# Bias and router loads moved to turn 7, the second half's entry and the router stretched, the experts moved by four slots

## The chip, the cores and the metric

The kernel runs on one core of one Trainium2 chip. A core has engines that run beside each other, each taking its own queue of instructions in order: TensorE (PE: matmuls and transposes; its weight loads are listed apart as PEld), VectorE (DVE), ScalarE (ACT) and GpSimd (POOL). SyncE (SP) does no arithmetic here; it issues every DMA of the kernel, also in order. An instruction that has to wait for a semaphore holds up everything behind it in its own queue. The metric is the time of one execution on the device in microseconds (us); lower is better.

## What is computed

Four sequences of 256 tokens with 256 features go through two residual layers. The first is a gated delta net, a linear attention computed in chunks; the second is a mixture of experts. Cut to what matters:

```
x = x + layernorm(attn(layernorm(x)))      # four sequences of 256 tokens, 256 features
x = x + layernorm(moe(layernorm(x)))

attn: q, k, v, z  = x @ W_qkvz             # 16 query/key heads, 32 value heads, 128 wide
      b, a        = x @ W_ba
      q, k, v     = silu(causal_conv4(...))
      beta, g     = sigmoid(b), -exp(A_log) * softplus(a + dt_bias)
      for each chunk of a head:
          T      = inverse(I + stril(k_beta @ k.T * decay))
          v_new  = T @ v_beta - (T @ (k_beta * exp(g))) @ state
          out    = (q * exp(g)) @ state + (q @ k.T * decay) @ v_new
          state  = state * exp(g_last) + (k * exp(g_last - g)).T @ v_new
      out = (norm_w * rmsnorm(out) * silu(z)) @ W_out

moe:  p     = softmax(x @ router_w + router_b)
      gates = top 6 of 32, scaled to sum 1
      out   = mean of 2 shared experts + sum over gates of gate * expert(x)
      expert(x) = relu(x @ w1 + b1) @ w2 + b2       # 256 -> 176 -> 256
```

## The kernel before, in words

All arithmetic is in 32-bit floats. The attention is cut into 32 **units**: unit u is one query/key head with its two value heads, over two of the four sequences. Units 0 to 15 cover the first half of the tokens, 16 to 31 the second half. A unit goes through stages written as Python generators:

- `weights` issues the loads of the projection weights `w`, of `wz` (gate) and of `wo` (output projection).
- `decays` loads the unit's cumulated gates, tile `gw`, from the DRAM tensor `g_rows` (L301), one copy to all partitions. POOL adds a mask (L307) and ACT takes exponentials (L317).
- `prepare` does the projection (`pj`, L357), the convolution on DVE (L367), transposes for the norms, and the products `pk` (L409, L433), which DVE combines with `gw` into the tile `am` (L413, L436). It then writes the diagonal 16 x 16 blocks of `am` to DRAM as `mb`, eight DMAs (L453).
- `blocks`, once for two units (u odd), reads these back as `wm` (L474), inverts them on DVE, writes the result to DRAM as `db` (L522), and loads it into the tiles `diag[0]` and `diag[1]`, one for each unit, eight DMAs each (L528). In the profile the two tiles have one name, `diag`.
- `solve` builds the inverse of the unit's matrices from these blocks on PE (`py`, `pd`, `pdT`, L545). Its first matmul, `py<-diag,e`, waits for the unit's `diag`.
- `gate` and `finish` compute `pz`, the solution `pu` and `pm`, the output `po`, its norm, the transposes `pth`, and the projection `pp` (L690), which DVE adds to `acc`.

Beside the units run five other stages. `entry(h)` normalises half h of the tokens, transposes it into `xT` (`pt_a`), computes the gates from `pba`, and writes them to `g_rows` (L260). `small` loads the router's weights `rw` and `rb`, the expert biases `b2s`, and the biases `b1`. The last come in as `b_raw`, go out to a DRAM tensor `b1f` in another order, one element of 4 bytes at a time (128 x 34 in one DMA and 48 x 34 in another: 5,984 elements), and come back as `b1s` in two more DMAs. The read of `b1s` has to wait until both writes of `b1f` have landed. `post(h)` forms the residual, normalises it, transposes it into `xT` again and computes the router's gates, mostly on DVE. `experts(h)` runs over 47 groups of hidden features: matmul `ph` (L849), ACT's relu (L852), DVE's product with the gates (L858), matmul `py` (L869), and at its end the last norm and the store.

**The order of the work** is written out by hand. A turn is nine slots, `at(turn, slot) = turn * 9 + slot`, and unit u starts at `at(u, 0)`. Each `yield` in a stage names the place at which the instructions behind it are to stand, and a heap takes the stages' pieces in the order of their places. This fixes the queues of PE, ACT, DVE and POOL instruction by instruction. It says nothing of times: a piece with a later place stands further back in its engine's queue. SP's queue is ordered by the framework's own scheduler, from these places and its estimate of when a DMA can go; `tc.issue_after(x)` makes the DMAs of its block stand behind x in SP's queue. `places(start, step)` gives a stage with many pieces a place every `step` slots.

Tiles come from pools with few buffers, so a DMA into a tile may have to wait until the earlier content has been read. The expert weights `we` use the buffers of `am` (four), the products of gates and hidden features those of `gw`, and so on.

Of the kernel before, what the change touches and what calls it, by code (L numbers as in the profile page):

```python
# [17 lines left out]
HQK, HV, HD = 16, 32, 128  # L18
# [13 lines left out]
def at(turn, slot):  # L32
    return turn * SLOTS + slot
# [30 lines left out]
def gated_delta_net_moe(  # L64
# [26 lines left out]
    def bank(tag, shape, name):  # L91
        return psum.tile(shape, F32, tag=tag, name=name)
# [13 lines left out]
    def load_x(name, h):  # L106
        xns[h] = u1.tile([P, NL, D], F32, tag="xn", name=f"xn_{name}_{h}")
        nc.sync.dma_start(xns[h], tokens(x_in, h))
# [45 lines left out]
    def places(place, step):  # L154

        while True:
            yield place
            place += step

    def layernorm(at_, src, dst, eps, name, tiles=range(NL)):  # L160

        n = len(tiles)
        st = ln.tile([P, NL, 6], F32, tag="st", name=f"st_{name}")
        mv = ln.tile([P, NL, 2], F32, tag="mv", name=f"mv_{name}")
        rs = ln.tile([P, NL], F32, tag="rs", name=f"rs_{name}")
        for i, t in enumerate(tiles):
            yield next(at_)
            nc.vector.bn_stats(st[:, i, :], src[:, t, :])
            nc.vector.bn_aggr(mv[:, i, :], st[:, i, :])
        nc.vector.tensor_scalar(rs[:, :n], mv[:, :n, 1], eps, None, ALU.add)  # L170
        nc.gpsimd.tensor_tensor(rs[:, :n], rs[:, :n], nhalf[:, :n], ALU.pow)
        for i, t in enumerate(tiles):
            yield next(at_)
            nc.vector.tensor_scalar(
                dst[:, t, :], src[:, t, :], mv[:, i, 0:1], rs[:, i : i + 1], ALU.subtract, ALU.mult
            )

    def transposed(at_, src, h, name):

        for k in range(2):  # L180
            yield next(at_)
            pt = bank("ms", [P, NL, P], f"pt_{name}_{k}")
            for i in range(NL):
                nc.tensor.transpose(pt[:, i, :], src[:, i, k * P : (k + 1) * P], ident)
            nc.scalar.copy(xT[:, k, h * T : (h + 1) * T], pt.rearrange("p a b -> p (a b)"))
# [82 lines left out]
    state = [{} for _ in units]  # L268
# [436 lines left out]
    groups = [(i, min(P, nh - i)) for i in range(0, nh, P)]  # L705
# [13 lines left out]

    def small():  # L720

        yield at(3, 0)
        nc.sync.dma_start(rw, router_w.rearrange("(k p) e -> p k e", p=P))
        nc.sync.dma_start(rb, router_b.partition_broadcast(P))
        nc.sync.dma_start(b2s, b2)
        raw = u1.tile([P, 13, NL * HV // 2], F32, tag="temp", name="b1_raw")
        b1f = dram.tile([nh], F32, name="b1f")
        for i, rows in enumerate((slice(0, P), slice(P, DH))):
            n = rows.stop - rows.start
            nc.sync.dma_start(raw[:n, i, :NE], b1[rows, :])  # L730
            nc.sync.dma_start(b1f.rearrange("(e h) -> h e", h=DH)[rows, :], raw[:n, i, :NE])
        yield at(5, 0)
        full = nh // P
        nc.sync.dma_start(b1s[:, :full], b1f[: full * P].rearrange("(i p) -> p i", p=P))
        nc.sync.dma_start(b1s[: nh - full * P, full:], b1f[full * P :].rearrange("(i p) -> p i", i=1))

    def post(h, at_):

        tl = slice(h * NL, (h + 1) * NL)
        a = acc[:, tl, :]  # L740
        yield next(at_)
        load_x("b", h)
        xn = xns[h]
        yield from layernorm(at_, a, a, 1e-5, f"b_{h}")
        for i in range(2):
            yield next(at_)
            c = slice(2 * i, 2 * i + 2)
            nc.vector.tensor_tensor(a[:, c], xn[:, c], a[:, c], ALU.add)
        yield from layernorm(at_, a, xn, 1e-5, f"c_{h}")
        yield from transposed(at_, xn, h, f"c_{h}")  # L750
        yield next(at_)
        plg = bank("ms", [P, NL, NR], f"plg_{h}")
        for t in range(NL):
            for k in range(2):
                nc.tensor.matmul(
                    plg[:, t, :],
                    xT[:, k, h * T + t * P : h * T + (t + 1) * P],
                    rw[:, k, :],
                    start=(k == 0),
                    stop=(k == 1),  # L760
                )
        temp = u1.tile([P, 13, NL * HV // 2], F32, tag="temp", name=f"route_{h}").rearrange("p a b -> p (a b)")
        used = [0]

        def part(*shape):
            n = shape[0] * (shape[1] if len(shape) > 1 else 1)
            got = temp[:, used[0] : used[0] + n]
            used[0] += n
            return got.rearrange("p (a b) -> p a b", a=shape[0]) if len(shape) > 1 else got

        lg, pr, rest, gates, top = (part(NL, n) for n in (NR, NR + 2, NR + 2, NE, 8))
        mx, sm = part(NL), part(NL)
        nc.vector.tensor_tensor(lg, plg, rb.unsqueeze(1).to_broadcast([P, NL, NR]), ALU.add)
        yield next(at_)
        nc.vector.tensor_reduce(mx, lg, AX.X, ALU.max)
        nc.vector.tensor_tensor(lg, lg, mx.unsqueeze(2).to_broadcast([P, NL, NR]), ALU.subtract)
        yield next(at_)
        nc.scalar.activation(lg, lg, AF.Exp)
        yield next(at_)
        nc.vector.tensor_reduce(sm, lg, AX.X, ALU.add)  # L780
        nc.vector.reciprocal(sm, sm)

        nc.vector.memset(pr, -1.0)
        nc.vector.tensor_tensor(
            pr[:, :, :NR], lg, sm.unsqueeze(2).to_broadcast([P, NL, NR]), ALU.mult
        )
        yield next(at_)
        for t in range(NL):
            nc.vector.max(top[:, t, :], pr[:, t, :NR])
        nc.vector.memset(top[:, :, TOPK:], -1.0)  # L790
        yield next(at_)
        for t in range(NL):
            nc.vector.match_replace(rest[:, t, :], top[:, t, :], pr[:, t, :], 0.0)
        yield next(at_)
        nc.vector.tensor_tensor(gates[:, :, :NR], pr[:, :, :NR], rest[:, :, :NR], ALU.subtract)
        nc.vector.tensor_reduce(sm, gates[:, :, :NR], AX.X, ALU.add)
        nc.vector.reciprocal(sm, sm)
        nc.vector.tensor_tensor(
            gates[:, :, :NR], gates[:, :, :NR], sm.unsqueeze(2).to_broadcast([P, NL, NR]), ALU.mult
        )  # L800

        nc.vector.memset(gates[:, :, NR:], 1.0 / NS)
        yield next(at_)
        gTs[h] = u1.tile([NE, 2 * 3 * P], F32, tag="gr", name=f"gT_{h}")[:, :T]
        pgt = bank("ms", [NE, NL, P], f"pgt_{h}")
        for t in range(NL):
            nc.tensor.transpose(pgt[:, t, :], gates[:, t, :], ident)
        nc.scalar.copy(gTs[h], pgt.rearrange("p a b -> p (a b)"))
        nc.sync.dma_start(gate_rows[h], gTs[h])
# [7 lines left out]
    def experts(h, start):  # L817
# [56 lines left out]
                    stop=(i + 1 == n),  # L874
                )

        LAG, EARLY = 2, 12
        for i in range(-EARLY, n + LAG):
            yield start + i
            if 0 <= i + EARLY < n:  # L880
# [40 lines left out]
    def begin(place, stage):  # L921
        heapq.heappush(parts, (place + next(stage), len(begun), place, stage))
        begun.append(stage)

    stages = [
        entry(0, places(-9, 0.3), places(6.8, 0.1)),
        entry(1, places(at(6, 0), 0.7), places(at(10, 0), 0.7)),
        small(),
        post(0, places(at(HQK + 4, 6), 0.7)),
        experts(0, at(2 * HQK + 2, 0)),  # L930
        post(1, places(at(2 * HQK + 4, 5), 0.5)),
        experts(1, at(2 * HQK + 2, 0) + len(groups)),
    ]
    for stage in stages:
        begin(0, stage)
    for u in range(len(units)):
        for stage in [weights, decays, prepare, gate, finish, solve] + [blocks] * (u % 2):
            begin(at(u, 0), stage(u))

    E = mybir.EngineType  # L940
    with tc.manual_schedule(engines={E.PE, E.Activation, E.DVE, E.Pool}):
        while parts:
            _, number, place, stage = heapq.heappop(parts)
# [52 lines left out]
```

## Time and profile before

| | |
|---|---|
| median of 3 runs | 1556.27 us (1556.08 to 1556.82) |
| the profiled execution's own time | 1556.75 us |
| its span in the profile | 1554.9 us |
| PE busy | 1454.9 us, 94% of the span |
| DVE, ACT, POOL busy | 839.8, 867.0, 464.8 us |
| moved by DMA | 126.51 MB, 81 GB/s over the span |
| packets | 232329, of which 159190 under 512 B |

The page of the profile cuts the span into 40 slices of some 39 us. Units fill the first 28 of them or so; from there the experts join, and the last ten are theirs almost alone. The trace can be asked for a timeline of each engine, for windows (busy time of each engine in a stretch), for waits (who waited for whom, put down to the releaser that came last) and for the chain of waits that ended last.

### The profile page before, as it was taken

What the parts mean: (1) busy time and instruction counts of PE and PEld (TensorE: products, weight loads), DVE (VectorE), ACT (ScalarE), POOL (GpSimd) and SP (SyncE); (2) the same over time, 40 slices, a digit from 0 to 9 for tenths busy, and PEclk for the clock granted to TensorE, in tenths of its full rate; (3) what the DMA queues carried; (4) which work ended last, traced back from release to release, by engine and by line L of the source; (5) the groups of instructions that cost most, each with busy time, mean ns of one, the idle gap of its engine ahead of it and who ended that gap; (6) DMA issues with size and microseconds to landing.
All of it is one profiled execution on the core that took longest, in us unless ns stands there. A gap on an engine that the chain in (4) does not pass through costs nothing.

```text
span 1554.9 us, 30006 instructions
## 1 busy us (share of the span) xinstructions
PE 1454.9 (94%) x11652; PEld 1009.9 (65%) x11652; DVE 839.8 (54%) x1693; ACT 867.0 (56%) x2206; POOL 464.8 (30%) x306
## 2 busy tenths in 40 slices
PE   5459998999999999999999999999979999999997
PEld 3226766777777777777777777777866654444443
DVE  4375666566575756668775765767431224231212
ACT  4456667777677777766677777677523321222111
POOL 1132333343354334345424334345331110000000
PEclk8679999999999999999999999999989999999999
DMA  3521312232222323223222323223133455555521
GB/s 114 68 60 50 93 41 66 71 81 62 61 67 57 85 71 71 62 56 67 64 69 58 93 62 71 64 54 75 35 68 89 123 146 144 151 149 161 155 75 44
DMA packets 232329, 126.51 MB, mean 81 GB/s; under 512 B 159190, under 2 KB 201528, under 8 KB 232188
## 3 DMA queue, kind: packets, MB, share of 16 engines
q1 hardware_dynamic: 232188, 124.59, 31.2%
q8 instruction: 93, 1.52, 0.4%
q14 instruction: 48, 0.39, 0.1%
HBM read 116.82 MB, written 7.70 MB: 80 GB/s over the span
## 4 chain that ended last, share of the span: by engine, by line
PE 72%; DVE 11%; ACT 7%; DMA 4%; issue 3%; SPq 2%; POOL 0%; POOLq 0%; DVEq 0%; ACTq 0%
PE ph L849 10%; PE py L869 10%; PE pj L357 10%; PE pp L690 6%; PE pz L331 4%; PE pd L545 4%; PE pdT L545 4%; DVE c L367 3%; PE po L634 3%; PE py L545 3%; PE pk L409 3%; PE pu L621 3%; ACT junko L643 2%; PE po L638 2%; PE pk L433 2%
## 5 line engine op out<-in xcount | busy, mean ns | idle before, releaser
L367 DVE SCALAR_TENSOR_TENSOR c<-pj,cw,c 128x510 f32<-128x510 f32 (+2 forms) x384 | 286.1, 745 | 168.9 <-ACT c L365 159.8
L654 POOL TENSOR_TENSOR rs<-rs,nhalf 128x4 f32<-128x4 f32 x64 | 78.0, 1220 | 678.6 <-DVE rs L650 473.3
L357 PE MATMUL pj<-xT,w 128*128 128x512 f32 x512 | 250.3, 613 | 5.1 <-DVE c L367 5.0
L852 ACT ACTIVATE h<-ph,b1s 128x512 f32<-128x512 f32 (+1 forms) x94 | 64.6, 687 | 241.5 <-PE ph L849 241.3
L849 PE MATMUL ph<-xT,we 128*128 128x512 f32 (+1 forms) x376 | 177.6, 595 | 0.7 <-ACT d L586 0.7
L365 ACT ACTIVATE c<-pj,cw 128x512 f32<-128x512 f32 x128 | 87.5, 685 | 161.6 <-PE pj L357 161.6
L869 PE MATMUL py<-hg,we 128*128 128x512 f32 (+1 forms) x376 | 176.4, 593 | 0.0
L858 DVE TENSOR_TENSOR hg<-h,gb 128x512 f32<-128x512 f32 (+1 forms) x94 | 65.7, 700 | 175.5 <-ACT h L852 168.3
L553 POOL TENSOR_TENSOR e<-am,cst 64x1024 f32<-64x1024 f32 x64 | 151.0, 2359 | 2.4
L357 PEld LDWEIGHTS pj<-xT,w 128*128 128x128 f32 x512 | 96.1, 198 | 79.3 <-issue 75.5
L646 DVE TENSOR_TENSOR hm<-po,sz 128x512 f32<-128x512 f32 x64 | 43.9, 686 | 179.1 <-ACT junko L643 177.2
L869 PEld LDWEIGHTS py<-hg,we 128*128 128x128 f32 (+1 forms) x376 | 71.3, 190 | 90.5 <-issue 88.6
L690 PE MATMUL pp<-wo,hT 128*128 128x256 f32 x512 | 123.2, 384 | 3.6 <-ACT hT L685 3.6
L331 PE MATMUL pz<-wz,xT 128*128 128x256 f32 x512 | 122.1, 382 | 0.0
L849 PEld LDWEIGHTS ph<-xT,we 128*128 128x128 f32 (+1 forms) x376 | 69.4, 189 | 77.8 <-issue 76.2
L690 PEld LDWEIGHTS pp<-wo,hT 128*128 128x128 f32 x512 | 98.0, 192 | 32.8 <-ACT hT L685 17.0
L331 PEld LDWEIGHTS pz<-wz,xT 128*128 128x128 f32 x512 | 93.3, 192 | 10.7 <-issue 0.5
L409 PE MATMUL pk<-c 128*128 128x512 f32 x128 | 73.0, 653 | 29.0 <-DVE am L413 22.0
L413 DVE SCALAR_TENSOR_TENSOR am<-pk,br,gw 128x512 f32<-128x512 f32 x128 | 89.9, 743 | 18.7 <-ACT gw L317 17.7
L317 ACT ACTIVATE gw<-gw,ng 128x256 f32<-128x256 f32 (+1 forms) x256 | 98.7, 447 | 1.5 <-POOL gw L307 1.1
L643 ACT ACTIVATE junko<-po 128x128 f32<-128x128 f32 x256 | 70.9, 277 | 48.8 <-PE po L638 34.1
L307 POOL TENSOR_TENSOR gw<-gw,cst 128x1024 f32<-128x1024 f32 x32 | 75.5, 2358 | 49.3 <-DMA gw<-g_rows 49.3
(170 smaller groups left out, 2734.5 us busy)
## 6 DMA issues: line engine op xcount, KB each, us to landing
gw<-g_rows SPq DMA_DIRECT2D x32, 768.0 KB, 5.6
w<-in_w_qkvz SPq DMA_DIRECT2D x32, 512.0 KB, 4.9
we<-in_w SPq DMA_DIRECT2D x126, 128.0 KB, 2.6
gb<-gate_rows SPq DMA_DIRECT2D x34, 256.0 KB, 3.5
wz<-in_w_qkvz SPq DMA_DIRECT2D x32, 256.0 KB, 2.7
wo<-in_w_out SPq DMA_DIRECT2D x32, 256.0 KB, 2.7
mb<-am SPq DMA_DIRECT2D x256, 8.0 KB, 1.6
db<-dd SPq DMA_DIRECT2D x16, 256.0 KB, 2.0
```

The source lines that it names most:

```text
L317: nc.scalar.activation(y, y, AF.Exp, bias=ng[:, t, h : h + 1])
L331: nc.tensor.matmul(pz[:, j].rearrange("p r e -> p (r e)"), xT[:, k, t * P : (t + 1) * P], state[u]["wz"][:, k, :], start=(k == 0), stop=(k ...
L357: nc.tensor.matmul(pj.rearrange("p b s -> p (b s)"), state[u]["w"][:, k, col * P : (col + 1) * P], xT[:, k, bp * T : (bp + 1) * T], start= ...
L367: nc.vector.scalar_tensor_tensor(y[:, :, back:], pj[:, :, : S - back], cw[:, row, 3 - back : 4 - back], y[:, :, back:], ALU.mult, ALU.add,)
L409: nc.tensor.matmul(pk, s[:, 1, b * S : b * S + P], s[:, 0:2, b * S : (b + 1) * S], start=True, stop=True)
L413: nc.vector.scalar_tensor_tensor(am[:, r, b, 0:4, :].rearrange("p (i x) c -> p i (x c)", i=2), pk, br[:, 2 * b, r : r + 1], gw[:, r, b, 0: ...
L545: nc.tensor.matmul(po[g, h, :], lhsT[g, h, :], rhs[g, h, :], start=True, stop=True)
L553: nc.gpsimd.tensor_tensor(e[g], mt[g, :, g].unsqueeze(1).to_broadcast(full), lev[g].unsqueeze(2).to_broadcast(full), ALU.mult,)
L643: nc.scalar.activation(junk, po[:, b, r, :], AF.Square, accum_out=os_[:, x, b, r : r + 1])
L690: nc.tensor.matmul(pp[:, b, :], hT[:, b, r, :], state[u]["wo"][:, r, :], start=(r == 0), stop=(r == R - 1))
L849: nc.tensor.matmul(ph[:rows], w[:, k * P : k * P + rows], xT[:, k, c], start=(k == 0), stop=(k == 1))
L869: nc.tensor.matmul(py[m], w[:rows, 2 * P + m * P : 2 * P + (m + 1) * P], hgs[i // 3][:rows, i % 3 * T : (i % 3 + 1) * T], start=False, sto ...
```

## The change

Five things change. Places first: the loads of `small`, which stood at turn 3 (and the two reads of `b1s` at turn 5), now all stand at turn 7, and in SP's queue behind the read `wm` of unit 5's blocks. `entry(1)` keeps its start at turn 6 but takes 1.4 slots from piece to piece instead of 0.7, and its second part starts at turn 12 instead of turn 10. `post(0)` too takes 1.4 slots from piece to piece. Both halves of the experts start four slots later. The expert weights are issued ten slots ahead of their group instead of twelve. (`base` is a new name for an old value.)

```
     def small():
-        yield at(3, 0)
+        yield at(7, 0)
+        with tc.issue_after(state[5]["wm"].ins):
+            small_loads()
+
+    def small_loads():
         nc.sync.dma_start(rw, router_w.rearrange("(k p) e -> p k e", p=P))
         nc.sync.dma_start(rb, router_b.partition_broadcast(P))
         nc.sync.dma_start(b2s, b2)
...
             nc.sync.dma_start(raw[:n, i, :NE], b1[rows, :])
             nc.sync.dma_start(b1f.rearrange("(e h) -> h e", h=DH)[rows, :], raw[:n, i, :NE])
-        yield at(5, 0)
         full = nh // P
         nc.sync.dma_start(b1s[:, :full], b1f[: full * P].rearrange("(i p) -> p i", p=P))
         nc.sync.dma_start(b1s[: nh - full * P, full:], b1f[full * P :].rearrange("(i p) -> p i", i=1))
...
-        LAG, EARLY = 2, 12
+        LAG, EARLY = 2, 10
...
         entry(0, places(-9, 0.3), places(6.8, 0.1)),
-        entry(1, places(at(6, 0), 0.7), places(at(10, 0), 0.7)),
+        entry(1, places(at(6, 0), 1.4), places(at(12, 0), 1.4)),
         small(),
-        post(0, places(at(HQK + 4, 6), 0.7)),
-        experts(0, at(2 * HQK + 2, 0)),
+        post(0, places(at(HQK + 4, 6), 1.4)),
+        experts(0, at(2 * HQK + 2, 4)),
         post(1, places(at(2 * HQK + 4, 5), 0.5)),
-        experts(1, at(2 * HQK + 2, 0) + len(groups)),
+        experts(1, at(2 * HQK + 2, 4) + len(groups)),
     ]
...
     for u in range(len(units)):
+        base = at(u, 0)
         for stage in [weights, decays, prepare, gate, finish, solve] + [blocks] * (u % 2):
-            begin(at(u, 0), stage(u))
+            begin(base, stage(u))
```

## The prediction

> **What bounds the kernel now.** I read the page first, then the waits of TensorE (PE), then SyncE's (SP's) queue and the windows wherever PE is idle.
>
> The page's busy times and slices:
>
> ```profile
> PE 1454.9 (94%) x11652; PEld 1009.9 (65%) x11652; DVE 839.8 (54%) x1693; ACT 867.0 (56%) x2206; POOL 464.8 (30%) x306
> ...
> PE   5459998999999999999999999999979999999997
> ...
> PEclk8679999999999999999999999999989999999999
> ```
>
> PE is the bound, idle for 100 of 1554.9 us: in slices 1 to 3, slightly in 5 to 7 and 19 to 20, in slice 30, and at the tail. The change adds and removes no arithmetic, so it can only move these gaps, or open a new one.
>
> SP's queue at the start (start, us, line, operation):
>
> ```profile
> 35.59 0.37 SPq L260 DMA_DIRECT2D g_rows<-gr  x1
> ...
> 36.81 0.38 SPq L731 DMA_DIRECT2D b1f<-b_raw  x1
> 37.43 2.81 SPq L301 DMA_DIRECT2D gw<-g_rows  x2
> 40.34 7.42 SPq L731 DMA_DIRECT2D b1f<-b_raw  x1
> 63.94 0.36 SPq L734 DMA_DIRECT2D b1s<-b1f  x1
> 64.35 4.29 SPq L735 DMA_DIRECT2D b1s<-b1f  x1
> 68.69 3.98 SPq L453 DMA_DIRECT2D mb<-am  x8
> ```
>
> The bias scatter b1f (5,984 elements of 4 bytes in two DMAs) goes out 0.6 us ahead of unit 0's and 1's gates gw; b1s then waits for it until 63.94. Who waits for gw, from POOL's and PE's timelines:
>
> ```profile
> 57.52 2.34 POOL L307 TENSOR_TENSOR gw<-gw,cst 128x1024 f32<-128x1024 f32 x1 [49.27 <-DMA gw<-g_rows]
> ```
>
> ```profile
> 61.93 2.07 PE L409 MATMUL pk<-c 128*128 128x512 f32 x2 [19.75 <-DVE am L413]
> ```
>
> The chain of waits confirms it: gw holds the path from 37.43 for 19.95 us, against a median landing of 5.6 us.
>
> SP's queue around turn 7:
>
> ```profile
> 228.82 0.34 SPq L474 DMA_DIRECT2D wm<-mb  x1
> ...
> 241.82 0.37 SPq L283 DMA_DIRECT2D wz<-in_w_qkvz  x1
> 243.15 0.34 SPq L522 DMA_DIRECT2D db<-dd  x1
> 246.50 7.69 SPq L528 DMA_DIRECT2D diag<-db  x16
> ```
>
> Windows around entry(1), in a quiet stretch, and during post(0):
>
> ```profile
> 200.00:240.00 40.00, 35.23 (x313) 27.38 (x311) 29.42 (x62) 24.30 (x67) 12.62 (x8) 0.96 0.21 63
> 240.00:280.00 40.00, 36.47 (x341) 27.60 (x341) 25.49 (x48) 30.31 (x73) 15.51 (x10) 0.96 0.28 62
> 400.00:440.00 40.00, 40.00 (x415) 31.15 (x415) 24.13 (x45) 29.46 (x77) 18.89 (x12) 1.00 0.23 57
> 720.00:760.00 40.00, 38.40 (x405) 30.23 (x400) 33.80 (x65) 25.92 (x70) 19.18 (x13) 1.00 0.28 68
> 760.00:800.00 40.00, 36.37 (x347) 28.22 (x346) 31.58 (x79) 27.08 (x68) 14.15 (x9) 0.96 0.25 67
> ```
>
> After the length come the busy times of PE, PEld, DVE, ACT and POOL, the granted clock, DMA share and GB/s. A quiet turn has no idle PE, so whatever delays PE there is paid in full.
>
> **The change part by part.** The profiled execution took 1556.75 us (span 1554.9, 1.85 around it), 0.5 above the median of the runs; the sum is made against it.
>
> *The scatter leaves the start.* Nothing then stands ahead of gw. At the median landing of 5.6 us it arrives at 43.0 instead of 57.43: 14.4 us less. If it lands only with the second gw behind it (11.2), 8.8 less. Windows of 54 to 58 us show 170 and 378 GB/s while these two loads run freely, so I take 14. Everything up to 115 us follows from gw through POOL, ACT and DVE, so the gain passes on. rw, rb, b2s and b_raw held nothing there: g_rows went out as its copy ended. b1s's 4.3 us on SP ended at 68.64, when am was ready too, so their removal is worth nothing; the cover is DVE's am.
>
> *The scatter in turn 7.* In the built program SP's order there is: wm of blocks(5), gw, rw, rb, b2s, b_raw twice, w, b1f twice, wz, b1s twice, then db and the 16 diag. So db, on which the next solve hangs, is queued behind b1s, which waits for the whole scatter. Counted from wm's issue (t0): the small issues take 3.4 us; b_raw lands behind gw's 5.6, so b1f's elements start at about t0+8. Its length: at the start the first DMA's 4,352 elements held gw for 14.4 us, 3.3 ns each, so 19.8 us for all; both DMAs with the two gw between took 36.81 to 63.94, 27.1 us. I take 23.5, as gw ran freely for part of the 27. So b1s goes out at t0+31.5; from its issue to the queue's next one took 4.75 us (63.94 to 68.69), so db at t0+36.3. From db to PE's first complete py took 7.3 us at the start (107.72 to 114.98): py at t0+43.6. In undisturbed turns py starts 23.5 us (305.87 to 329.35) or 22.7 us (442.52 to 465.22) after wm; with a pt_a transpose placed ahead of it, 24. PE, which takes its queue in order, stalls 19.5 us (16 to 23 with the ends), and ACT, DVE and the later mb all wait for PE. After its long idle at the start the granted clock was 0.50 up to the window of 66 to 68 and 1.00 in that of 70 to 72, with PE restarted at 61.93; about 6 us at half speed cost 3 more. Together +22.5 (18 to 26.5). Nothing hides it: PE has no idle time to give.
>
> A rule speaks against this step. The Trainium skill (DMA: Bandwidth & Descriptors, Rules for kernel authors) says to issue a DMA early and wait on its semaphore late. The trace's 19.95 us of gw show what early cost here, but the wait right behind b1f in turn 7 is what the rule warns of; by the rule alone, early would be free, and the move would be worth +22.5 with no gain.
>
> The same skill (TensorE: Matmul & The Clock Gate, Why this matters for your kernels) has the clock fall after some 3 us of idle, and (Part 1: The HAM clock gate) come back after about 3.4 us of work. That would make the clock's term 1.7 instead of 3, an estimate from that page; the rows above decide.
>
> *entry(1) at half the pace.* The two windows from 200 to 280 lose 4.77 + 3.53 us idle and 2 x 40 x 0.04 = 3.2 us of clock: 11.5. TensorE's waits from 195 to 265 us name its operations: pt_a on xn_a 2.3, pba on xT 1.4, and pp on ACT's hT 2.2, while ACT loads entry(1)'s tables. With 1.4 slots between steps instead of 0.7, DVE and ACT meet half the extra work per turn, and what follows the stall finds them drained. Ends: 0 (the delays stay) and 11.5; near the second, I take 10, one such wait staying. Its second half moves two turns; PE, ACT and DVE then do the same work there, and g_rows is read only from unit 16 on (turn 15): nothing.
>
> *post(0) at half the pace.* The windows from 720 to 800 lose 1.6 + 3.63 idle and 1.6 of clock, 6.8 us. DVE is busy 65 us there, 20.6 in the quiet 800 to 840. Ends 0 and 6.8; I take 4.5, since its single DVE groups stay as long as they were.
>
> *Experts four slots later, their weights two slots later still.* SP's queue at the transition:
>
> ```profile
> 1136.04 0.33 SPq L522 DMA_DIRECT2D db<-dd  x1
> 1138.54 0.38 SPq L831 DMA_DIRECT2D we<-in_w  x1
> ...
> 1145.41 3.87 SPq L528 DMA_DIRECT2D diag<-db  x8
> ```
>
> Thirteen expert loads stand between db and diag, and py waits for diag until 1150.76 though its predecessor on PE ended at 1144.95. In the new order four stand there: 1.9 us, so diag at 1140.5, landed about 1.8 after its 3.87 us of issue, at 1146.1: 4.6 us less, and some 2 of the clock (it was 0.51 from 1150 to 1155). Against it, four slots of solve and finish lose the first expert matmuls as filler; the same steps of the unit before, unfilled, show waits of 0.69 and 0.53 us (pp on hT, pth on hm), so 1.2 to 3. Net -4 (-6.5 to +5). DVE and POOL keep their work, post(1) its places, the tail its order: nothing.
>
> Sum: -14 + 22.5 - 10 - 4.5 - 4 = -10, so 1546.7 against the profiled execution and 1546.2 against the median.
>
> **The rivals.** (1) *The turn 7 wait is hidden.* If the scatter, with less beside it on the DMA engines, takes 4 us or less, py comes at t0+24 (8 + 4 + 4.75 + 7.3) and the 22.5 falls away: 1524. For it: after the gw, the second DMA's 1,632 elements had landed within some 7 us. Against: that is about 4 ns each, and 5,984 of them 24 us.
>
> (2) *Slower.* The scatter drains more slowly among turn 7's traffic than at the start, and PE stands at the same py for longer. Its price: the second DMA's 1,632 elements landed 23.6 us after their issue, two gw ahead of them included, so 14 ns each is an upper bound; at 7 ns the scatter takes 41.9 us and PE's loss grows by 18.4: 1564.6. It decides from where the stall and the clock cost 36 us (the gains of 32.5 and 3.1 more), which is a scatter of 37 us, 6.2 ns an element. For it: while the first one drained, gw's loads crawled at 14 to 38 GB/s, so each slows the other. Against: the 27.1 us at the start held two loads of 768 KB already, and turn 7 has one such ahead of it and a w of 512 KB.
>
> (3) *No change.* Should the 14 and the stall stand, but the spread steps give only half (7) and the transition nothing, the sum is +1.5: 1557.8, which cannot be told from the median; 0.2% is 3.1 us, about what a measurement can tell from no change.
>
> **How the numbers follow.** The forecast has 0.60 (own range 1538 to 1552), rival 1 0.12, rival 2 0.18, rival 3 0.10. Faster: 0.60 + 0.12 = 0.72; within 0.2%: 0.10; slower: 0.18. The range reaches from 1533 (rival 1's upper part: a stall of 9 to 10) to 1561 (rival 3, and rival 2 up to 6.5 ns an element).
>
> **What would show it.** gw landing 5 to 7 us after its issue, with the wait of pk on am near 6 instead of 19.75; in turn 7 b1s issued some 31 us after wm and one PE wait of py on diag near 20 us, clock 0.50 behind it; windows at entry(1) and post(0) nearly full; py's last long wait on diag at the transition about 1 us. The prediction is wrong if SP passes b1s without a wait of over 10 us, if PE's startup gap shrinks less than the gw wait, or if the four slots ahead of the experts show more than 5 us of idle PE.

## The result, and the profile after

The changed kernel takes 1556.2 us (median of 12 runs, 1551.84 to 1560.57), the kernel before 1555.15 in the runs beside it (median of 12). The ratio is 1.0007, with a 95% interval of 0.9994 to 1.0019: no difference. The forecast was 1546.2. The profiled execution took 1558.12 us with a span of 1556.3, 1.4 more than the span before.

The page of the changed kernel, TensorE's (PE's) busy time and its slices and clock:

```profile
PE 1459.9 (94%) x11652; PEld 1015.6 (65%) x11652; DVE 845.7 (54%) x1693; ACT 866.3 (56%) x2206; POOL 463.0 (30%) x306
...
PE   5668996999999999999999999999989999999997
...
PEclk9779998999999999999999999999989999999998
```

Slices 2 and 3 are fuller than before (6 and 6 in place of 4 and 5), slice 7 has become a hole (6, with the clock at 8, in place of 8 and 9), and the last slices look alike. So something was gained early and given back at about 250 us. To put numbers on it, both traces can be read at one landmark, the start of each unit's second key product on PE (pk_2, line 433). An undisturbed turn takes 33.6 us:

| stretch, by pk_2 of units | before, us | after, us | difference |
|---|---|---|---|
| start to unit 4 | 180.7 | 166.7 | -14.0 |
| unit 4 to 9 (scatter, entry(1)) | 184.6 | 199.3 | +14.7 |
| unit 9 to 12 (entry(1)'s second part) | 101.0 | 105.0 | +4.0 |
| unit 12 to 19 | 235.2 | 235.2 | 0 |
| unit 19 to 24 (post(0)) | 179.2 | 179.8 | +0.6 |
| unit 24 to 31 | 233.4 | 233.2 | -0.2 |
| unit 31 to the end (transition, experts) | 440.8 | 437.1 | -3.7 |

The differences add up to the 1.4 us of the spans. The start and the transition went as forecast; the stretch from unit 4 to 12 cost 18.7 more than before where the forecast had +12.5 (22.5 for the scatter less 10 for entry(1)'s pace), and post(0) gave nothing.

**The start.** SyncE's (SP's) queue, then POOL's and PE's rows that wait for gw (start, us, engine, line, operation; in brackets the idle time before it and what ended it):

```profile
35.17 0.35 SPq L260 DMA_DIRECT2D g_rows<-gr  x1
37.01 0.89 SPq L301 DMA_DIRECT2D gw<-g_rows  x2
53.67 3.65 SPq L453 DMA_DIRECT2D mb<-am  x8
```

```profile
42.52 2.34 POOL L307 TENSOR_TENSOR gw<-gw,cst 128x1024 f32<-128x1024 f32 x1 [34.21 <-DMA gw<-g_rows]
```

```profile
46.93 2.08 PE L409 MATMUL pk<-c 128*128 128x512 f32 x2 [5.03 <-DVE am L413]
```

Nothing stands between g_rows and gw any more; gw lands within 5.5 us of its issue instead of 19.95, and PE waits 5.03 us instead of 19.75.

**Turn 7.** SP's queue from wm, on the path of the next solve, to diag, which that solve needs:

```profile
213.41 0.34 SPq L474 DMA_DIRECT2D wm<-mb  x1
...
219.97 3.05 SPq L735 DMA_DIRECT2D b1f<-b_raw  x2
223.11 6.53 SPq L283 DMA_DIRECT2D wz<-in_w_qkvz  x1
241.20 0.36 SPq L737 DMA_DIRECT2D b1s<-b1f  x1
241.61 3.48 SPq L738 DMA_DIRECT2D b1s<-b1f  x1
245.19 0.38 SPq L522 DMA_DIRECT2D db<-dd  x1
```

and PE's rows at the end of it, with windows behind them (length, busy us of PE, PEld, DVE, ACT, POOL, granted clock, DMA share, GB/s):

```profile
238.65 1.14 PE L599 MATMUL pdl<-phi,y_l 64*64 64x64 f32 x16
250.78 0.44 PE L545 MATMUL py<-diag,e 64*64 64x64 f32 x2 [10.98 <-DMA diag<-db]
252.67 1.93 PE L545 MATMUL py<-diag,e 64*64 64x64 f32 x30 [1.45 <-DMA diag<-db]
```

```profile
245.00:250.00 5.00, 0.00 (x0) 0.00 (x0) 0.00 (x0) 0.00 (x0) 0.26 (x1) 0.50 0.44 66
250.00:255.00 5.00, 2.77 (x33) 2.53 (x34) 0.36 (x1) 0.00 (x0) 0.00 (x0) 0.50 0.36 34
255.00:260.00 5.00, 5.00 (x16) 3.42 (x16) 2.68 (x6) 0.00 (x0) 0.00 (x0) 0.82 0.13 19
```

b1s goes out 27.8 us after wm, db 31.8 after, and PE stands for 12.4 us at py, all other engines with it. The clock is at 0.50 until well after PE has restarted.

**Around entry(1) and post(0)** the windows should have been nearly full. They are not:

```profile
280.00:320.00 40.00, 36.32 (x334) 27.87 (x333) 31.09 (x60) 27.14 (x70) 14.49 (x9) 0.94 0.20 59
...
400.00:440.00 40.00, 37.48 (x359) 29.05 (x358) 24.46 (x44) 28.27 (x73) 19.50 (x12) 1.00 0.19 52
...
760.00:800.00 40.00, 36.82 (x352) 28.92 (x351) 30.55 (x64) 25.53 (x68) 15.22 (x10) 0.95 0.20 58
```

The first two are new losses, at places that were full before; the third is as it was.

**The transition.** SP's queue and PE's longest wait there:

```profile
1140.70 0.33 SPq L522 DMA_DIRECT2D db<-dd  x1
1142.78 0.38 SPq L834 DMA_DIRECT2D we<-in_w  x1
...
1144.70 8.80 SPq L528 DMA_DIRECT2D diag<-db  x16
```

```profile
1151.09 1.92 PE L545 MATMUL py<-diag,e 64*64 64x64 f32 x30 [1.69 <-DMA diag<-db]
```

Four expert loads instead of thirteen stand between db and diag, and py's wait is 1.69 us.

### The profile page after: what moved, and what is told of

Read it like the earlier page. It is cut to its first block, busy times and chain, and to the rows that moved or that the text cites. A ratio compares the mean times of both kernels' runs of the same rounds, so it can differ in the third digit from the quotient of the medians.

```text
span 1556.3 us, 30025 instructions
## 1 busy us (share of the span) xinstructions
PE 1459.9 (94%) x11652; PEld 1015.6 (65%) x11652; DVE 845.7 (54%) x1693; ACT 866.3 (56%) x2206; POOL 463.0 (30%) x306
## 3 DMA queue, kind: packets, MB, share of 16 engines
q1 hardware_dynamic: 232188, 124.59, 31.3%
## 4 chain that ended last, share of the span: by engine, by line
PE 69%; DVE 12%; ACT 6%; DMA 6%; SPq 3%; issue 3%; POOL 1%; POOLq 0%; DVEq 0%; ACTq 0%
PE ph L852 10%; PE py L872 10%; PE pj L357 9%; PE pp L690 5%; PE pd L545 4%; PE pdT L545 4%; PE pz L331 4%; DVE c L367 3%; PE po L634 3%; PE py L545 3%; PE pk L409 2%; PE pu L621 2%; ACT junko L643 2%; PE pk L433 2%; PE po L638 2%
## 5 line engine op out<-in xcount | busy, mean ns | idle before, releaser
L634 PE MATMUL po<-ut,am 128*128 128x128 f32 x512 | 91.1, 292 | 0.0
L634 PEld LDWEIGHTS po<-ut,am 128*128 128x128 f32 x512 | 76.8, 201 | 17.5 <-issue 15.3
```

The lines of the kernel that those rows point to most:

```text
L634: nc.tensor.matmul(po[:, b, r, :], am[:, r, b, x, :], ut[:, 0, b, r, :], start=True, stop=(x == 0))
```

## The experiments

The forecast's terms are A, the scatter leaving the start; B, the scatter in turn 7; C, entry(1) at half the pace; D, post(0) at half the pace; E, the experts four slots later. The ratios are to the kernel before, with 95% intervals. "Excess" is what a stretch takes beyond 33.6 us a turn in the profiled execution.

**One part at a time.** First the changed kernel with the small loads back where they were, and the kernel before with one of the other edits alone:

```
 # small loads back:       small() as before (turn 3 and turn 5), the rest as changed
 # entry alone:
-        entry(1, places(at(6, 0), 0.7), places(at(10, 0), 0.7)),
+        entry(1, places(at(6, 0), 1.4), places(at(12, 0), 1.4)),
 # post alone:
-        post(0, places(at(HQK + 4, 6), 0.7)),
+        post(0, places(at(HQK + 4, 6), 1.4)),
 # experts alone:           at(2 * HQK + 2, 4) for both halves, EARLY = 10
```

> The changed kernel with the small loads put back where they stood before (the scatter at the start, no wait in turn 7); the two slower paces and the later experts stay. The forecast's terms C, D and E (-10, -4.5, -4) make 18.5 us less than before: ratio 0.988. Rival theory, from the trace of the changed kernel: the slower paces only spread the same delays over more turns (entry(1) +3, post(0) +0.6) and only the transition gains (-3.7): no difference from before, ratio 1.000. In the trace the forecast wants turns of about 34 us from unit 5 to 9; the rival wants excesses of 1 to 6 us in four or five turns there.

> The kernel before with entry(1) alone at 1.4 slots a step and its second half at turn 12. Forecast: 10 us less, ratio 0.9936. Rival (spread, not saved): between 0 and 3 us more, ratio 1.000 to 1.002. A third theory, that the pace does help but the stall in turn 7 takes the gain back, wants about -10 here too and wants it lost only beside the stall.

> The kernel before with post(0) alone at 1.4 slots a step. Forecast: 4.5 us less, ratio 0.997. Rival (spread, not saved): +0.6, ratio 1.0004, with the same 11 us of excess spread over four turns in place of three.

> The kernel before with the experts four slots later and their loads ten groups ahead in place of twelve, nothing else. Forecast's term E: 4 us less, ratio 0.9974, with py's wait on diag at the transition falling from 4.0 us to about 1. Rival: the four slots without filler cost what the wait gives back: ratio 1.000, with waits of pp and pth of 3 us or more in the last attention turns.

| kernel | ratio | excess, unit 4 to 9 | unit 9 to 12 | unit 19 to 24 | unit 31 to end, us |
|---|---|---|---|---|---|
| before | 1 | 16.6 | 0.2 | 11.2 | 440.8 |
| changed | 1.0007 | 31.3 | 4.2 | 11.8 | 437.1 |
| small loads back | 0.9989 (0.9980 to 0.9997) | 11.0 | 4.3 | 11.8 | 436.9 |
| entry alone | 1.0013 (1.0003 to 1.0023) | 11.3 | 4.2 | 11.2 | 439.3 |
| post alone | 0.9985 (0.9974 to 0.9997) | 15.4 | 0.4 | 8.5 | 439.4 |
| experts alone | 0.9984 (0.9975 to 0.9993) | 16.4 | 0.3 | 9.6 | 436.9 |

C, D and E together gave 1.7 us (0.0011 of 1556), where the forecast had 18.5. Entry alone is 2 us slower, not 10 faster. Its trace shows the two halves of this: the first part saves 5 us between units 4 and 9, the second part costs 4 more between 9 and 12. (1.3 of the 5 are the second part's, which in the kernel before had begun in the turn of unit 9. The 2 us themselves are partly the start: its unit 4 begins at 182.9 us, that of before at 180.7, and the edit touches nothing there.) Post alone saves 2.3 of 4.5. The experts alone save 2.5 by the times and 3.9 by the trace: the 4 of the forecast lie at the upper end of the interval (1.1 to 3.9).

Where the first part's gain went is seen in PE's waits between units 5 and 7. In the kernel before:

```profile
227.03 0.65 PE L184 MATMUL pt_a<-cst,xn_a 128*128 128x128 f32 x2 [2.26 <-DVE xn_a L174]
234.33 2.00 PE L200 MATMUL pba<-wba,xT 128*128 128x64 f32 x16 [1.43 <-ACT xT L185]
252.66 2.75 PE L690 MATMUL pp<-wo,hT 128*128 128x256 f32 x8 [2.16 <-ACT hT L685]
260.30 1.12 PE L409 MATMUL pk<-c 128*128 128x512 f32 x2 [1.36 <-ACT junk L388]
```

With entry(1) alone at 1.4 slots:

```profile
237.11 0.27 PE L545 MATMUL pd<-y,dT 64*64 64x64 f32 x1 [2.47 <-DVE y L568]
250.00 0.66 PE L684 MATMUL pth<-cst,hm 128*128 128x128 f32 x4 [0.23 <-POOL hm L656]
251.57 1.12 PE L409 MATMUL pk<-c 128*128 128x512 f32 x2 [0.92 <-DVE am L413]
```

and its windows from unit to unit, beginning with unit 5:

```profile
217.00:254.90 37.90, 34.27 (x343) 26.50 (x341) 30.55 (x65) 24.64 (x67) 15.77 (x11) 1.00 0.29 69
254.90:292.50 37.60, 36.25 (x361) 28.07 (x357) 21.81 (x40) 30.26 (x74) 13.49 (x10) 1.00 0.25 66
292.50:328.70 36.20, 33.85 (x340) 26.05 (x337) 29.37 (x59) 25.29 (x67) 13.16 (x10) 1.00 0.30 72
...
395.90:433.50 37.60, 35.09 (x351) 26.97 (x347) 22.68 (x40) 26.71 (x69) 17.24 (x11) 1.00 0.21 52
```

The waits on entry(1)'s own tiles are gone, and a wait that the kernel before had not there, pd on y, has come: one big gap has become four, of 3.6, 1.4, 2.4 and 2.5 us, and only the drop of the clock is saved. y itself comes sooner than in the kernel before, 19.4 us after unit 5's pk_2 in place of 22.5. PE waits for it because PE is no longer held at pt_a and pba ahead of it. What y then hangs on can be followed back, since DVE takes its list in order:

```profile
220.50 0.41 DVE L168 BATCH_NORM_STATS2 st_a<-xn_a 128x6 f32<-128x256 f32 x1
220.94 0.18 DVE L169 BATCH_NORM_AGGREGATE mv_a<-st_a 128x2 f32<-128x6 f32 x1
221.04 1.63 DVE L436 SCALAR_TENSOR_TENSOR am<-pk,br,gw 128x256 f32<-128x256 f32 x4
...
232.00 0.39 DVE L174 TENSOR_SCALAR xn_a<-xn_a,mv_a,rs_a 128x256 f32<-128x256 f32 x1 [0.81 <-issue]
...
233.43 0.69 DVE L646 TENSOR_TENSOR hm<-po,sz 128x512 f32<-128x512 f32 x1 [1.04 <-ACT junko L643]
...
236.37 0.68 DVE L568 TENSOR_TENSOR y<-py,cst 128x512 f32<-128x512 f32 x1
```

```profile
231.53 0.42 ACT L480 ACTIVATE dd<-wm 128x256 f32<-128x256 f32 x1 [2.68 <-DMA wm<-mb]
```

Between hm and y stands the first part of the block inverse. The step of entry(1) ahead of hm, xn_a, costs y nothing that shows: behind it DVE is idle for another 1.04 us, until ACT's junko (part of the norm of po). ACT came late to junko because it had waited 2.68 us for wm, the blocks read back from DRAM; wm was issued late (12.4 us after pk_2, 10.0 in the undisturbed turn of unit 11 before) because mb had been written late, and mb waits for am. In front of am stand st_a and mv_a of entry(1), twice, for 0.6 us each time, and a step of the unit, qe, that takes 1.36 us in place of 0.16. So am starts 4.1 us after pk_2, and 1.8 in that undisturbed turn. The changed kernel shows the same chain: am at 4.1 us, 2.90 us of ACT's wait for wm, 2.70 of PE's for y.

**What of the scatter holds turn 7.** Three kernels. One issues b1s two turns later, behind wm of blocks(7), so that db is not queued behind it; one keeps every instruction and place but writes b1f as its rows lie; one does the latter in the kernel before, where it is the start that should answer:

```
 # b1s late (changed kernel):
+        yield at(9, 0)
+        with tc.issue_after(state[7]["wm"].ins):
+            (the two loads of b1s)
 # plain rows (changed kernel), and plain rows (kernel before):
-            nc.sync.dma_start(b1f.rearrange("(e h) -> h e", h=DH)[rows, :], raw[:n, i, :NE])
+            nc.sync.dma_start(b1f.rearrange("(h e) -> h e", e=NE)[rows, :], raw[:n, i, :NE])
```

> The changed kernel with the two loads of b1s issued two turns later, behind the wm of blocks(7), so that nothing in turn 7 waits for the scatter; the scatter itself stays in turn 7. If the wait of db behind b1s is the cost (12.4 us of one PE wait and some 3 of half clock), the time is 14 to 16 us below the changed kernel: ratio about 0.990 of before. Rival: the stall covered delays of entry(1) that come back when it is gone: 6 to 9 us below the changed kernel, ratio 0.995. Second rival: the scatter itself slows diag and wm among the DMA engines, so that db still lands late: less than 5 us, ratio 0.997 or more.

> The changed kernel with b1f written as its rows lie (176 rows of 136 bytes) in place of 5,984 single elements of 4 bytes; so the biases come out in another order and the output is not the reference's. Every instruction, wait and place stays. If the scattered elements are what holds turn 7, py's wait on diag there falls from 12.4 us to under 1.5 and the time by 16 to 20: ratio about 0.989 of before. If SP's order is the cause (b1s waiting for b1f, whatever its form, with db behind it), most of the wait stays: ratio 0.996 or more. If the stall only covered entry(1)'s own delays, they come back: about 10 us less, ratio 0.994.

> The kernel before with b1f written as its rows lie, so that only the scatter's elements are gone: every load keeps its place at the start, and the biases come out in another order (the output is not the reference's). Term A by itself: if the scattered elements held gw, gw lands 5 to 9 us after its issue in place of 19.95, unit 0's keys start some 14 us earlier and the time falls by 14 to 17: ratio 0.989 to 0.991. If instead the place in the queue counts (two loads and a write ahead of gw, whatever their form), gw still lands late and the ratio is 0.996 or more.

b1s late: 0.9978 (0.9965 to 0.9990), 4.5 us under the changed kernel (1.0007) where 14 to 16 were expected. Its SP queue and PE:

```profile
231.27 3.84 SPq L522 DMA_DIRECT2D db<-dd  x1
245.17 7.70 SPq L528 DMA_DIRECT2D diag<-db  x16
```

```profile
248.76 0.45 PE L545 MATMUL py<-diag,e 64*64 64x64 f32 x2 [9.07 <-DMA diag<-db]
```

db is issued 14 us earlier than in the changed kernel, and diag, which waits for it, only 2 us earlier: 13.9 us from one to the other, against 3.35 in the kernel before. PE's wait falls from 12.4 us to 10.2. So it is the scatter itself that holds db, and SP's order was worth 2 us of it in the trace (4.5 by the times).

Plain rows in the changed kernel: 0.9880 (0.9862 to 0.9898), 20 us under it, and no wait of py on diag among PE's waits between 195 and 300 us. Unit 4 to 9 has an excess of 14.4 in place of 31.3. Plain rows in the kernel before: 0.9913 (0.9895 to 0.9931), 13.5 us less. POOL's row there:

```profile
42.97 2.34 POOL L307 TENSOR_TENSOR gw<-gw,cst 128x1024 f32<-128x1024 f32 x1 [34.70 <-DMA gw<-g_rows]
```

gw has the same place in the queue, behind b_raw and the first b1f, and lands within 5.5 us. At both places the 5,984 single elements were the cost, not the two DMAs.

**One queue, or the DMA engines?** The scatter in ACT's own queue, with b1s late; first three slots into turn 7, then earlier:

```
-            nc.sync.dma_start(b1f.rearrange("(e h) -> h e", h=DH)[rows, :], raw[:n, i, :NE])
+            nc.scalar.dma_start(b1f.rearrange("(e h) -> h e", h=DH)[rows, :], raw[:n, i, :NE])
 # first run at (7, 3); second run at (6, 8.3), its loads at (6, 5.6)
```

> The kernel with b1s issued late (db not behind it), and the scatter b1f issued by ACT into its own DMA queue, 3 slots after turn 7's start. If db landed late there because its packets stood behind the scatter's elements in SP's queue, they now pass them: py's wait on diag under 2 us, ratio about 0.989 of before. If the DMA engines themselves are taken up by the scatter, whatever the queue, db still lands some 10 us late: ratio 0.997, as with one queue.

> The scatter in ACT's own DMA queue again, but issued some 15 us earlier than in the first such run, so that it runs beside db and the diag loads of turn 7 (b1s issued late, as there). If db was late because its packets stood behind the scatter's in one queue, db and diag now pass: py's wait on diag under 1.5 us and, with the gates' temp tile free earlier, a time of 1541 to 1544, ratio 0.990. If the DMA engines are the shared thing, db and diag crawl beside it as they do in one queue: py waits 8 to 11 us, ratio 0.996 or more.

The first run does not answer: ACT came to the scatter only at 235.9, when the diag loads had passed, so it ran beside nothing that matters. Its ratio is 0.9933 (0.9914 to 0.9951), and it shows another cost, in DVE's row of entry(1)'s gates:

```profile
257.68 0.29 DVE L213 TENSOR_TENSOR temp<-pba,dtb 128x128 f32<-128x128 f32 x1 [7.05 <-DMA diag<-db]
```

The releaser named had long been done; what landed at 257.5 was b1f (issued 236.4, 21.1 us), and its source b_raw shares the tile temp with entry(1). So entry(1) waited for the scatter, PE lost 4.0 us behind it, and even behind all other loads of the turn the scatter took 21.6 us (235.9 to 257.5).

The second run answers. Its scatter is issued from 218.64 on, and SP's queue and ACT's read:

```profile
226.50 0.34 SPq L522 DMA_DIRECT2D db<-dd  x1
241.12 8.73 SPq L528 DMA_DIRECT2D diag<-db  x16
```

```profile
218.64 10.43 ACTq L745 DMA_DIRECT2D b1f<-b_raw  x2
...
229.11 0.60 ACT L338 ACTIVATE sz<-pz 128x512 f32<-128x512 f32 x1 [7.81 <-PE pth L684]
```

db again takes 14.6 us to its diag, with the scatter in another queue: the queue does not matter, and what the two share lies behind the queues. Whether that is the DMA engines or the DRAM that both write to, these runs do not tell apart. The ratio is 0.9968 (0.9956 to 0.9979), as the second theory had it. py's wait is only 2.1 us because PE is late by then: issuing the scatter held ACT up for 10 us (the row before sz is that issue, whatever releaser is named), and PE waits 3.1 us for hT.

The trace's packets tell how: counted in stretches of 2 us in this run, with the mean time that one of them took,

```
from us   4-byte packets, each     2,048-byte packets, each
222       1995,   10 ns            142,   84 ns   (w)
226       1041,   44 ns              2,  635 ns
228       1059,   27 ns             33,  638 ns   (db)
230        232,   85 ns             33,  710 ns   (db)
232        317,   55 ns             27,  657 ns   (db)
```

The elements start out at 10 ns each and come to 27 to 85; db's packets take 635 to 710 ns, and 437 and 201 in the next two stretches, in which the elements run out. In the changed kernel, where db goes out after the scatter has landed, its 128 packets take 85 ns each.

**Taking the scatter away for good.** Two transposes on PE turn the biases (128 + 48 rows of 34 become 34 rows of 176), ACT copies them out, and b1f is written in 34 rows of 704 bytes two turns later, b1s read four turns later. Once with the changed kernel's paces, once with entry(1) as before (the biases six turns later, for the tile that they share):

```
+        pt = bank("ms", [P, DH], "pt_b1")
+        for i, rows, n in parts_:
+            nc.tensor.transpose(pt[:NE, rows], raw[:n, i, :NE], ident[:n, :n])
+        turned = u1.tile([NE, 2 * 3 * P], F32, tag="gr", name="b1_turned")[:, :DH]
+        nc.scalar.copy(turned, pt[:NE])
...
+            nc.sync.dma_start(b1f.rearrange("(e h) -> e h", h=DH), turned)
```

> The changed kernel with the biases turned by two PE transposes and one ACT copy, then written as 34 rows of 704 bytes two turns later and read by b1s four turns later: no scatter anywhere. The start's gain (15 to 17 us), entry(1)'s 1.3, post(0)'s up to 2.7 and the transition's 3.7 stay and the stall's 16 to 20 go: 16 to 22 us below both kernels, ratio 0.986 to 0.990. Rival: the reading of b1s element by element (5,984 of 4 bytes) blocks the queue as the scatter did, in turn 11: ratio 0.996.

> The same with entry(1) at the pace of before (0.7 slots, second half at turn 10) and the turned biases six turns later. The forecast's term C wants this 10 us slower than the run with turned biases and 1.4 slots (ratio 0.993 to 0.997); the reading from the traces (251.9 against 250.6 us over six turns) wants it 1 us slower, which can't be told from none.

Turned biases: 0.9885 (0.9868 to 0.9901), 18 us under the kernel before. With entry(1) at the old pace: 0.9902 (0.9885 to 0.9918). The medians differ by 2.0 us, where term C wanted 10; with turned biases too, half the pace is worth next to nothing.

**Pace or place?** If the place of single steps in DVE's order decides, the place of entry(1) should matter more than its pace. Only the first place of entry(1) is changed, in the kernels with turned biases:

```
 # two later, four later (pace 1.4):  places(at(6, 2), 1.4)   places(at(6, 4), 1.4)
 # four later (pace 0.7):             places(at(6, 4), 0.7)
```

> The run with turned biases, with entry(1)'s first half two slots later (same 1.4 slots a step). If term C gained so little because single steps of entry(1) stand ahead of the solve's y in DVE's order, then other places meet y differently: the two waits of pd on y (4.6 us with the clock's drop behind the second) change, and the time with them by 3 us or more in either direction; two slots later should take them away, ratio 0.985 to 0.987. If the cost is only how much DVE and ACT have to do in a turn, moving it by two slots changes under 1.5 us: ratio 0.988 to 0.989.

> The run with turned biases, with entry(1)'s first half four slots later at 1.4 slots a step. If the place against y decides, the excess of turns 6 to 9 (14 us at no shift, with a drop of the clock in it, 8 us at two slots) moves again by 3 us or more, with other waits of pd, pk or pp. If the sum of the work decides, it stays within 2 us of the 10 to 11 us that the undisturbed runs at this pace show: ratio 0.987 to 0.989.

> The run with turned biases at the pace of before (0.7 slots), entry(1)'s first half four slots later. At no shift this pace costs 16 us over turns 5 to 9, most of it in one gap of 7 us with the clock's drop behind it. If the place decides, four slots take the gap to another wait and the excess changes by 4 us or more, either way: ratio 0.986 to 0.988, or 0.992 and above. If the pace's load decides, it stays at 15 to 17 us: ratio 0.990.

| entry(1)'s pace | slots later | ratio | excess, unit 4 to 9 | unit 9 to 12 |
|---|---|---|---|---|
| 1.4 | 0 | 0.9885 (0.9868 to 0.9901) | 15.3 | 4.2 |
| 1.4 | 2 | 0.9876 (0.9862 to 0.9889) | 8.2 | 4.2 |
| 1.4 | 4 | 0.9895 (0.9877 to 0.9913) | 7.7 | 4.2 |
| 0.7 | 0 | 0.9902 (0.9885 to 0.9918) | 16.1 | 1.1 |
| 0.7 | 4 | 0.9849 (0.9833 to 0.9866) | 6.6 | 0.9 |

At the old pace, four slots take the excess from 16.1 to 6.6, and the ratio falls by 0.0053, 8 us (some 3 us in the trace are the clock, 0.93 over unit 5's turn in the first and 1.00 in the second). That is the place deciding, not the load: the same steps at the same pace. In both kernels four slots later unit 5's am starts 1.8 us after pk_2, where it is 4.1 at no shift and 1.4 slots and 6.6 at no shift and 0.7; ACT no longer waits for wm in that turn, and PE waits for y 0.79 and 1.21 us. PE's two longest waits in the last of these kernels, from unit 5 to 7, and its window:

```profile
218.23 0.27 PE L545 MATMUL pd<-y,dT 64*64 64x64 f32 x1 [1.21 <-DVE y L568]
235.03 1.13 PE L409 MATMUL pk<-c 128*128 128x512 f32 x2 [0.71 <-DVE temp L213]
```

```profile
199.30:237.90 38.60, 36.58 (x365) 28.73 (x360) 30.95 (x69) 28.21 (x72) 18.52 (x12) 1.00 0.33 82
```

At the slow pace the traces show a gain with the shift too (15.3 to 8.2 and 7.7, some of it a drop of the clock in the turn of unit 7 that the first of these executions had, 0.91 over the turn, and the others not), but the ratios do not resolve it: their intervals overlap. For that pace it stays open. The stretch from unit 9 to 12 does not depend on the shift: 4.2 us at 1.4 slots and turn 12, about 1 at 0.7 and turn 10.

The kernel with turned biases, entry(1) at the old pace four slots later, post(0) at half its pace and the experts four slots later is the fastest found: 1530.74 us (1528.26 to 1533.11), 1.5% under both kernels.

## Why the prediction was wrong

**A, "The scatter leaves the start", -14: right.** 14.0 us by unit 4, gw landing at 42.5 against 43.0 worked out; the plain rows in the kernel before give 13.5 by the times.

**B, "The scatter in turn 7", +22.5: near in size, half right in mechanism.** Against the run with the small loads back (11.0 from unit 4 to 9) the changed kernel's 31.3 make it 20.3; the times of plain rows say 20. Of its parts, the stall was over-sized, 12.4 us instead of 19.5: b1s went out at t0+27.8 instead of t0+31.5, as the scatter began at t0+6.6 and took 21.2 us, not at t0+8 and 23.5, and PE came to py only at t0+26.4, not t0+24, because it had lost 2.7 us to a late y. From db to the complete py it was 7.5 us, worked out as 7.3. The 3 us of clock came about: the window of 255 to 260 puts the return of the full clock near 256.8, six us after PE's restart, as taken. The other 4.9 us the sum did not have: 2.2 lie around the stall and 2.7 in the turn of unit 7, where the clock was 0.91. The run with turned biases shows the same 0.91 there with no scatter at all, so these 2.7 need not be the scatter's. That the total came within 2.2 us of the forecast is partly luck: a stall 7 us too large and 5 us that were not foreseen. The Trainium skill (TensorE: Matmul & The Clock Gate, Part 1: The HAM clock gate) has the full clock back after about 3.4 us of sustained work. The six us here do not speak against it: behind the first two py PE waited again, for 1.45 us, and from the thirty that follow (252.67) it is 4.1 us. What the step had wrong is the cause: "db ... is queued behind b1s" named SP's order, and SP's order was worth some 2 us (4.5 by the times). With db in front, it crawled beside the scatter, from either queue.

Two rules of the Trainium skill would have told this, and were not used (DMA: Bandwidth & Descriptors, Rules for kernel authors): a last dimension that is not contiguous becomes one descriptor per element, and spreading DMAs over issuing engines does not help, since all run on the same 16 DMA engines. The runs agree with both: 20 us for the first, and for the second the 14.6 us from db to diag with the scatter in another queue, though where behind the queues the two meet no run shows. The rule that was weighed, issue early and wait late, does not settle this case: by it alone the early place was free, and it cost 14 us.

**C, "entry(1) at half the pace", -10: the step that failed most.** It came to -1.5 by the traces (15.3 against 16.8 of excess from unit 4 to 12). Two mistakes. The window's whole 11.5 us were taken as saved but for 1.5, since "DVE and ACT meet half the extra work per turn". But what PE waits for hung on the place of single steps in the order of DVE: in the changed kernel st_a and mv_a still stand ahead of unit 5's am, and 3.4 us of the gates' steps (temp) ahead of unit 7's. With the waits on pt_a and pba gone, PE came to the waits behind them, for the y that follows from each am (2.70 and 1.95 us). That the place decides is shown at the old pace: four slots later gained 8 us without any change of pace. For the slow pace it is read from the rows; the ratios there do not settle it. And "its second half moves two turns ... nothing" was wrong: that half takes 4.2 us where it took some 1.5 (1.3 of that in the turn of unit 9, still counted in the stretch before). PE waits there 1.66 us for am at pk, 0.61 at pg and 0.25 at another pk. Whether its pace or its turn did that was not tried apart.

**D, "post(0) at half the pace", -4.5: failed.** +0.6 in the changed kernel; alone, -2.7 in the trace and -2.3 (0.5 to 4.0) by the times. The step took the gaps as saved, and they were spread: in the four turns from unit 20 on PE is idle for 4.5 us before (nearly all of it in two turns) and for 4.1 in the run with post alone (in all four). Half of the forecast at best, and whether even that shows depends on the clock: in the six executions at this pace in which the turn of unit 21 shows 0.91, the stretch from unit 19 to 24 has an excess of 11.7 to 12.4, in the six in which it shows 1.00 one of 8.5 to 10.0. At the old pace it was 11.2 with a clock of 0.96 there (three executions) and 9.6 with 1.00 (one). Without the drop, the pace is worth a microsecond or less.

**E, "Experts four slots later", -4: right**, -3.7 in the trace, with py's wait at 1.7 us.

So A, B and E stand within some 2 us each and nearly cancel: -14.0 + 20.3 - 3.7 = +2.6. The whole forecast gain rested on C and D, 14.5 us, and they gave 0.9 (1.5 and -0.6). Rival 1 (the scatter hidden) and rival 2 (one of more than 37 us) are both out, with a scatter of 21.2 us and a stall of 12.4. The end is near rival 3's 1557.8, though by another way: the spread gave less than its half, the transition its 4. Of the three conditions listed for the prediction being wrong none came about, because none of them tested C or D. Of the signs listed for its being right, the nearly full windows at entry(1) and post(0) did not come.

## What to carry to other kernels

Look at what a DMA is made of before asking when to issue it: 5,984 elements of 4 bytes cost 14 us at one place and 20 at another and held db from either queue, and as rows they cost nothing that could be seen at the start and at most some 3 us in turn 7 (an excess of 14.4 against 11.0 with the loads at the start); turning 24 KB on PE first was worth 18 us. Idle time in a window is not a load that spreading halves: find which single instruction stands ahead of which in the order of its engine, follow the chain behind it (here through a write to DRAM and back), and move that. A wait that ends may only uncover the one behind it. And where a forecast rests on one term, write down what in the trace would refute that term.

## What the runs showed that was not expected

- The scatter lasts some 21 us with or without much beside it (21.2 in turn 7, 21.6 behind the diag loads), though its first half goes out at 7 to 13 ns a packet; later packets take up to 143 ns each (means of 2 us). What slows them is not settled. In the run with b1s late, the window below has packets that add up to 2.08 times the DMA engines' time (they overlap), at 6 GB/s:

```profile
228.00:232.00 4.00, 4.00 (x28) 2.71 (x27) 2.14 (x3) 2.83 (x12) 0.00 (x0) 1.00 2.08 6
```

- A wait of PE of 2.23 us (pd on y at 792.95, in the run with the small loads back) was followed by a clock of 0.50 in the window of 795 to 800; one of 2.47 us (the same wait at 237.11, in the run with entry(1) alone) was followed by none: 1.00 in all windows of 5 us from 230 to 250. The same wait so costs 2 us or 5, and whole stretches differ by 3 us from one execution to another of kernels that are the same there.
- The time of the start varies by itself where the scatter stands in it: unit 0's pk_2 begins between 64.8 and 66.6 us in the five kernels that have it there, and between 49.8 and 50.8 in all others.
